# Moving the sums of the state and the split of the first h from GpSimd to VectorE and ScalarE, in a gated graph network with an attention layer behind it

## Chip, cores, metric

One core of a Trainium2 chip. The metric is the device time of one run in microseconds (us).

## The reference, cut

64 graphs of 256 nodes with 256 features. Per graph: layer norm and ReLU, three gated steps, a residual sum, layer norm and ReLU again, one attention layer, a residual sum.

```python
h = jnp.maximum(_layernorm(x), 0.0)
for i in range(3):                                   # gated steps
    m = jnp.einsum('bnd,de->bne', h, weight[i])
    aggr = jnp.einsum('bst,bsd->btd', A, m)          # A: the adjacency, 0 or 1
    h = gru(aggr, h)                                 # two products with 256 x 768, sigmoid, tanh
x = x + h
h = jnp.maximum(_layernorm(x), 0.0)
hW = jnp.einsum('bnd,od->bno', h, W)
e = leaky((hW @ a_left)[:, :, None] + (hW @ a_right)[:, None, :])
x = x + softmax(where(A == 0, -1e9, e)) @ hW
```

## The kernel before

Two graphs are one pair; 32 pairs, of which up to three are in flight. Each operation is recorded with an engine and a guessed duration. A list scheduler then places them one by one, the one that can start first in its model first, by deadline where several can, and issues them in that order. Each engine has its own list, so the scheduler fixes who stands behind whom; the chip decides how long each takes. `pool` and `dve2` (VectorE operations with two inputs in SBUF, among others) are marked: in its model the scheduler never lets one of each run at the same time. Nothing makes the chip keep the modelled times, and in the trace they do overlap.

A product with the gate weights is done with seven half-size products in place of eight (Strassen-Winograd), which needs sums of quarters of its right factor. The right factors are h ("the sums of the state") and the aggregate; the first were on GpSimd, the others on VectorE:

```python
def right_factors(eng, op, b):
    T = Buf("full")
    c = (1195, 605, 605) if eng is nc.gpsimd else (V512, V256, V256)
    def first():
        q = quarters(b)
        eng.tensor_sub(T.t[:, : 2 * N].rearrange("p (c n) -> p c n", c=2), q[:, :, 1, :],   # L381
                       b.t[:, : 2 * N].rearrange("p (c n) -> p c n", c=2))
    op(c[0], first, ...)
    op(c[1], lambda: eng.tensor_sub(quarter(T, T2), quarter(b, B22), quarter(T, T1)), ...)  # L385
    op(c[2], lambda: eng.tensor_sub(quarter(T, T4), quarter(T, T2), quarter(b, B21)), ...)  # L387
    return T
```

The aggregate is a product of rounded tiles: h = hi + lo, both rounded, times the adjacency (L521 on TensorE, evicted by ScalarE at L525). For the first h the split was GpSimd's; for later ones it comes out of PSUM, hi by ScalarE (L583), lo by VectorE (L585).

```python
pool(530, lambda ...: nc.gpsimd.tensor_copy(nodes(hi)[:, sl, :], nodes(h)[:, sl, :]), ...)       # L504
pool(1190, lambda ...: nc.gpsimd.tensor_sub(nodes(lo)[:, sl, :], nodes(h)[:, sl, :],
                                            nodes(hi)[:, sl, :].bitcast(F32)), ...)                # L506
for i in range(L):
    Th = right_factors(nc.gpsimd, pool, hT)
    ...                                               # L521, L525: the aggregate
    Tg = right_factors(nc.vector, dve2, agT)
    ...                                               # products L413, evictions L420, additions L423
    dve2(...)   # L551  u = (u + b) * r       two SBUF inputs
    dve2(...)   # L554  u = u + u'            two SBUF inputs
    act(...)    # L556  tanh
    dve2(...)   # L558, L559, L561  h = (h - u) * z + u, in place
    ...         # L575 transposes of the new h; L583, L585 its split
```

In the attention layer, per pair: transposes of the softmax (L644), eviction by VectorE (L648), a product (L653), eviction by ScalarE (L657), the last projection (L662), all in the same lists as the gated steps of the two pairs behind it. The changed kernel is two lines shorter above these, so L662 is L660 there, L551 is L549, and so on.

## Time and profile before

| | before |
|---|---|
| time, median of 3 | 2404.17 us (2400.3 to 2406.48) |
| span of the profiled run | 2403.4 us |
| steady pair | 73.03 us, repeated within 0.01 |
| TensorE / VectorE / ScalarE / GpSimd busy | 98 / 73 / 56 / 22% |

A busy share of TensorE says little of what a change is worth. The useful count is this: take the distance from the end of one matrix instruction to the end of the next, subtract the usual distance of its kind (the prediction gives the three); what is left is a stop, with what the first instruction behind it loses. Below, "stop" always means this number, and stops per steady pair are means over 20 pairs. Lines from the profile before stand in the prediction.

### The profile page before, as it was taken

The numbers are of one execution on the slowest core, as the hardware profiler recorded it, in microseconds if no ns is written. First come the engines' busy times: TensorE is split into PE (matmuls) and PEld (weight loads), VectorE is DVE, ScalarE is ACT, GpSimd is POOL, SyncE is SP. The second block draws the span as 40 slices with busy tenths as digits, with TensorE's granted clock in tenths as the row PEclk, the third lists the DMA queues.
The fourth block names the chain that finished last, engine by engine and source line by source line (L and its number), as shares of the span: only waits on it lengthen the run. The fifth ranks groups of instructions, "written<-read, shape, count | busy, mean of one in ns | idle before, by whom it ended". The sixth has DMA issues, their size and how long they took to land.

```text
span 2403.4 us, 32216 instructions
## 1 busy us (share of the span) xinstructions
PE 2352.6 (98%) x12129; PEld 2068.3 (86%) x12129; DVE 1746.6 (73%) x3736; ACT 1352.0 (56%) x2627; POOL 520.3 (22%) x582
## 2 busy tenths in 40 slices
PE   8999999999999999999999999999999999999997
PEld 6878888888888888888888888888888888888885
DVE  5577776787777786777877767877777867778666
ACT  5455555556555556455555555565555564556554
POOL 3031222221222211222212222212222112222110
PEclk9999999999999999999999999999999999999998
DMA  3010000000000000000000000000000000000000
GB/s 114 1 36 1 27 27 27 27 18 10 27 27 27 27 9 18 27 27 27 27 1 27 27 27 27 18 10 27 27 27 27 6 22 27 27 19 9 1 9 18
DMA packets 53564, 55.03 MB, mean 23 GB/s; under 512 B 1680, under 2 KB 53408, under 8 KB 53408
## 3 DMA queue, kind: packets, MB, share of 16 engines
q1 hardware_dynamic: 53376, 52.96, 6.6%
q8 instruction: 96, 1.57, 0.3%
q14 instruction: 60, 0.49, 0.1%
q10 hardware_dynamic: 32, 0.01, 0.0%
HBM read 36.18 MB, written 16.78 MB: 22 GB/s over the span
## 4 chain that ended last, share of the span: by engine, by line
PE 88%; DVE 8%; ACT 3%; issue 0%; DMA 0%; POOL 0%; ACTq 0%; DVEq 0%
PE bank L413 69%; PE bank L521 8%; PE bank L662 5%; PE bank L575 3%; DVE full L551 3%; ACT full L556 2%; DVE full L554 1%; DVE full L648 1%; PE bank L482 1%; PE bank L644 1%; ACT full L657 1%; PE bank L611 1%; PE bank L653 1%; PE bank L345 0%; DVE full L423 0%
## 5 line engine op out<-in xcount | busy, mean ns | idle before, releaser
L413 PE MATMUL bank<-full,fac_hh 128*128 128x256 f32 x4032 | 1002.3, 379 | 0.6 <-ACT full L486 0.2
L413 PE MATMUL bank<-full,fac 128*128 128x256 f32 x4032 | 992.0, 379 | 0.0
L413 PEld LDWEIGHTS bank<-full,fac 128*128 128x128 f32 x4032 | 753.8, 190 | 96.6 <-DVE full L385 0.7
L413 PEld LDWEIGHTS bank<-full,fac_hh 128*128 128x128 f32 x4032 | 747.2, 190 | 93.6 <-DVE full L423 0.6
L423 DVE TENSOR_TENSOR full<-full,bank 128x512 f32<-128x512 f32 x576 | 379.9, 681 | 406.8 <-PE bank L413 349.4
L420 ACT COPY full<-bank 128x512 f32<-128x512 f32 x576 | 327.1, 584 | 283.7 <-PE bank L413 283.6
L381 POOL TENSOR_TENSOR full<-full 128x512 f32<-128x512 f32 x96 | 129.7, 1351 | 1204.5 <-DVE full L561 772.4
L537 ACT ACTIVATE full<-full,b_rz 128x512 f32<-128x512 f32 x192 | 131.5, 716 | 204.2 <-DVE full L423 203.9
L521 PE MATMUL bank<-round,round 128*128 128x256 f32 x1536 | 242.9, 301 | 3.4 <-DVE round L585 2.8
L521 PEld LDWEIGHTS bank<-round,round 128*128 128x128 f32 x1536 | 205.1, 190 | 21.7 <-issue 11.5
L462 POOL TENSOR_TENSOR small<-small,nhalf 128x2 f32<-128x2 f32 x128 | 91.8, 726 | 554.3 <-DVE small L460 552.6
L556 ACT ACTIVATE full<-full,vec 128x512 f32<-128x512 f32 x192 | 135.0, 723 | 100.5 <-DVE full L554 98.6
L525 ACT COPY full<-bank 128x512 f32<-128x512 f32 x192 | 112.6, 587 | 138.3 <-PE bank L521 138.3
L469 ACT ACTIVATE full<-x,small 128x256 f32<-128x256 f32 x256 | 136.6, 593 | 65.1 <-DVE small L464 65.0
L551 DVE SCALAR_TENSOR_TENSOR full<-full,vec,full 128x512 f32<-128x512 f32 x192 | 166.7, 895 | 7.2
L554 DVE TENSOR_TENSOR full<-full 128x512 f32<-128x512 f32 x192 | 141.1, 761 | 1.3
L662 PE MATMUL bank<-wT,full 128*128 128x256 f32 x512 | 118.6, 385 | 19.2 <-ACT full L657 19.2
L662 PEld LDWEIGHTS bank<-wT,full 128*128 128x128 f32 x512 | 95.0, 190 | 42.2 <-ACT full L657 30.4
L561 DVE TENSOR_TENSOR full<-full,full 128x512 f32<-128x512 f32 x192 | 127.7, 692 | 2.1
L559 DVE TENSOR_TENSOR full<-full,full 128x512 f32<-128x512 f32 x192 | 127.6, 690 | 1.3
L558 DVE TENSOR_TENSOR full<-full,full 128x512 f32<-128x512 f32 x192 | 127.3, 689 | 0.4 <-ACT full L556 0.4
L583 ACT CAST round<-bank 128x512 fp32r<-128x512 f32 x128 | 69.6, 594 | 101.0 <-PE bank L575 101.0
(79 smaller groups left out, 2282.6 us busy)
## 6 DMA issues: line engine op xcount, KB each, us to landing
x<-in_x_dram SPq DMA_DIRECT2D x32, 512.0 KB, 3.3
adj<-in_adj_dram SPq DMA_DIRECT2D x32, 512.0 KB, 3.3
out_dram<-x SPq DMA_DIRECT2D x32, 512.0 KB, 2.9
full<-in_L_gnn_w_ih_dram SPq DMA_DIRECT2D x2, 384.0 KB, 5.3
full<-in_L_gnn_weight_dram SPq DMA_DIRECT2D x3, 256.0 KB, 7.0
full<-in_L_gnn_w_hh_dram SPq DMA_DIRECT2D x2, 384.0 KB, 6.7
full<-in_L_gnn_W_dram SPq DMA_DIRECT2D x1, 256.0 KB, 7.2
rows<-in_L_gnn_a_dram ACTq DMA_DIRECT2D x1, 2.0 KB
```

Of the source, the lines that this page charges most:

```text
L381: eng.tensor_sub(T.t[:, : 2 * N].rearrange("p (c n) -> p c n", c=2), q[:, :, 1, :], b.t[:, : 2 * N].rearrange("p (c n) -> p c n", c=2))
L413: nc.tensor.matmul(bank.t[:, ts(s, N)], fac[t[0]][:, f, t[1], :], quarter(srcs(t), q), start=(first and n == 0), stop=True, skip_group_che ...
L420: act(A512, lambda: nc.scalar.copy(quarters(dest[e])[:, :, g, :], both(X)), r=[(X, ONE)], w=[(dest[e], (g, 2 + g))])
L423: dve(V512, lambda: nc.vector.tensor_add(quarters(dest[e])[:, :, g, :], quarters(dest[e])[:, :, g, :], both(bank)), r=[(bank, ONE)], w=[(d ...
L469: act(495, lambda k=k, nb=nb: nc.scalar.activation(nodes(dst)[:, k, :], nodes(src)[:, k, :], AF.Relu, bias=sm.t[:, 18 + nb : 19 + nb], sca ...
L521: nc.tensor.matmul(pa.t[:, ts(db, N)], nodes(part)[:, k, ts(db, P)], Ar()[:, k, :], start=(n == 0), stop=(n == len(terms) - 1))
L537: act(630, lambda s=s, RZ=RZ: nc.scalar.activation(feats(RZ[0])[:, s, :], feats(RZ[0])[:, s, :], AF.Sigmoid, bias=b_rz[:, 2 * s : 2 * s + 1]),
L551: dve2(660, lambda u=u, db=db, en=en, RZ=RZ: nc.vector.scalar_tensor_tensor(u(), u(), b_h[:, en : en + 1], feats(RZ[db])[:, 0, :], op0=ALU ...
L554: dve2(V512, lambda u=u, b=U[db]: nc.vector.tensor_add(u(), u(), feats(b)[:, 1, :]), r=[(U[db], (2, 3))], w=[(U[db], (0, 1))])
L556: act(630, lambda u=u, en=en: nc.scalar.activation(u(), u(), AF.Tanh, bias=b_i[:, en : en + 1]), r=[("vec", ONE)], w=[(U[db], (0, 1))])
L561: dve2(V512, lambda u=u, d=d: nc.vector.tensor_add(d(), d(), u()), r=[(U[db], (0, 1))], w=[(hT, q)])
L662: nc.tensor.matmul(pv.t[:, ts(ib, D)], ag.t[:, db * N + ib * P : db * N + (ib + 1) * P], wT[:, db, :], start=(db == 0), stop=(db == DB - 1))
```

## The change

GpSimd should keep only the power operation of the layer norm and a fill; its first sum takes 1351 ns in the mean, VectorE's of the same size 684.

```diff
-    def right_factors(eng, op, b):
+    def right_factors(b):
         T = Buf("full")
-        c = (1195, 605, 605) if eng is nc.gpsimd else (V512, V256, V256)
...
-            eng.tensor_sub(T.t[:, : 2 * N]...
+            nc.vector.tensor_sub(T.t[:, : 2 * N]...
-        op(c[0], first, ...)
+        dve2(V512, first, ...)
...   (the other two sums likewise)
-            pool(530, lambda ...: nc.gpsimd.tensor_copy(nodes(hi)..., nodes(h)...
+            act(630, lambda ...: nc.scalar.copy(nodes(hi)..., nodes(h)...
-            pool(1190, lambda ...: nc.gpsimd.tensor_sub(
+            dve2(V512, lambda ...: nc.vector.tensor_sub(
...
-            Th = right_factors(nc.gpsimd, pool, hT)
+            Th = right_factors(hT)
-            Tg = right_factors(nc.vector, dve2, agT)
+            Tg = right_factors(agT)
```

Every engine's list is scheduled anew from these durations.

More of the change, by code (lines that the diff above doesn't have):

```diff
@@ L373, in tile_gated_gnn_then_gat @@
     quarter = lambda b, q: b.t[:, q * N : (q + 1) * N]
-    def right_factors(eng, op, b):
+    def right_factors(b):
         T = Buf("full")
-        c = (1195, 605, 605) if eng is nc.gpsimd else (V512, V256, V256)
         def first():
             q = quarters(b)
-            eng.tensor_sub(T.t[:, : 2 * N].rearrange("p (c n) -> p c n", c=2), q[:, :, 1, :],
+            nc.vector.tensor_sub(T.t[:, : 2 * N].rearrange("p (c n) -> p c n", c=2), q[:, :, 1, :],
                            b.t[:, : 2 * N].rearrange("p (c n) -> p c n", c=2))
-        op(c[0], first, r=[(b, (B11, B12, B22))], w=[(T, (T1, T3))])
-        op(c[1], lambda: eng.tensor_sub(quarter(T, T2), quarter(b, B22), quarter(T, T1)),
+        dve2(V512, first, r=[(b, (B11, B12, B22))], w=[(T, (T1, T3))])
+        dve2(V256, lambda: nc.vector.tensor_sub(quarter(T, T2), quarter(b, B22), quarter(T, T1)),
            r=[(b, (B22,)), (T, (T1,))], w=[(T, (T2,))])
-        op(c[2], lambda: eng.tensor_sub(quarter(T, T4), quarter(T, T2), quarter(b, B21)),
+        dve2(V256, lambda: nc.vector.tensor_sub(quarter(T, T4), quarter(T, T2), quarter(b, B21)),
            r=[(b, (B21,)), (T, (T2,))], w=[(T, (T4,))])
@@ L503, in pair @@
             sl = slice(g * NB, (g + 1) * NB)
-            pool(530, lambda sl=sl, hi=hi, h=h: nc.gpsimd.tensor_copy(nodes(hi)[:, sl, :], nodes(h)[:, sl, :]),
+            act(630, lambda sl=sl, hi=hi, h=h: nc.scalar.copy(nodes(hi)[:, sl, :], nodes(h)[:, sl, :]),
                  r=[(h, ks)], w=[(hi, ks)])
-            pool(1190, lambda sl=sl, hi=hi, lo=lo, h=h: nc.gpsimd.tensor_sub(
+            dve2(V512, lambda sl=sl, hi=hi, lo=lo, h=h: nc.vector.tensor_sub(
                 nodes(lo)[:, sl, :], nodes(h)[:, sl, :], nodes(hi)[:, sl, :].bitcast(F32)),
```

## The prediction

> **What bounds the kernel now.** I read the page first: busy shares, then the slices.
>
> ```profile
> PE 2352.6 (98%) x12129; PEld 2068.3 (86%) x12129; DVE 1746.6 (73%) x3736; ACT 1352.0 (56%) x2627; POOL 520.3 (22%) x582
> ...
> PE   8999999999999999999999999999999999999997
> DVE  5577776787777786777877767877777867778666
> ```
>
> TensorE is busy in all slices but the first and last. VectorE has some 650 us free, GpSimd 1880 us. So taking work off GpSimd frees no engine that sets the time; the change can only gain where TensorE stands still or starts late. I therefore ask what the change is worth at those places alone. Next view: the chain that ended last, in order of time, in one steady pair of graphs (the loop runs 32 pairs).
>
> ```profile
> 1033.08 0.68 DVE full L648
> 1033.76 2.34 DVE full L551 x2
> 1036.10 1.15 DVE full L554
> ...
> 1037.92 0.72 ACT full L556
> 1038.65 0.48 ACT full L657
> 1039.13 0.04 issue
> 1039.17 3.72 PE bank L662 x16
> ...
> 1049.12 28.49 PE bank L413 x132
> ```
>
> The last line gives TensorE's undisturbed pace: 28.49/132 = 0.216 us per 256-column matrix instruction. From the individual records I took the distance from one end to the next for every line (0.216 us for 256 columns of fp32, 0.119 for the products of the rounded tiles at L521, 0.109 for transposes at 128) and added up what lies above the median: 71.8 us in all, so a perfect TensorE stream would take some 2332 us. By stretches of 73.05 us, the length of one pair: 7.5, 4.0 and 7.3 us in the first three; 1.21 us in each of the next 27; about 1 us in each of the next two; 19.5 us in the tail. Of the 1.21 us, 0.96 stands at L662 (0.69 idle, then a first instruction that is 0.27 longer), 0.25 at L521. Hence the ceiling: 27 to 28 steady pairs hold about 34 us, the start 19, the tail 19.5. The view of who waited for whom agrees:
>
> ```profile
> PE bank L662 <- ACT full L657: 19.2, 28, 0.7
> ```
>
> The wait's cause is further back: the eviction L657 stands on ScalarE behind two tanh (L556), which wait for VectorE's L551 and L554. Timeline of that spot, after a clean spot from earlier in the same pair:
>
> ```profile
> 1005.14 1.41 DVE L551 SCALAR_TENSOR_TENSOR full<-full,vec,full 128x512 f32<-128x512 f32 x2
> 1006.47 1.28 DVE L554 TENSOR_TENSOR full<-full 128x512 f32<-128x512 f32 x2
> ```
>
> ```profile
> 1033.67 2.42 DVE L551 SCALAR_TENSOR_TENSOR full<-full,vec,full 128x512 f32<-128x512 f32 x2
> ...
> 1034.16 1.38 POOL L381 TENSOR_TENSOR full<-full 128x512 f32<-128x512 f32 x1 [14.68 <-ACT full L486]
> ...
> 1035.62 1.06 POOL L385 TENSOR_TENSOR full<-full,full 128x256 f32<-128x256 f32 x1
> 1036.02 1.81 DVE L554 TENSOR_TENSOR full<-full 128x512 f32<-128x512 f32 x2
> ```
>
> The same two pairs of instructions take 2.69 us in the clean spot, 4.1 beside GpSimd's sums of the first h. That is the finding the prediction rests on. Sorting all records by overlap with GpSimd: L551 takes 748 ns alone (136 times), 1251 with overlap (56); L554 684 alone, 1172 with overlap (30). L423, which reads one operand from PSUM, takes 682 and 680: no difference.
>
> **What the Trainium skill says.** "SBUF — State Buffer", section "SBUF: two separate sides": GpSimd and VectorE share a port pair that is "an exclusive lock, not a bandwidth split", against VectorE operations with two SBUF inputs or in a two-port mode. The trace agrees: L551 and L554 (two SBUF inputs) stretch by 0.5 us, L423 (one PSUM input) not. "GPSIMD Engine Reference", section "Elementwise — side-by-side cycle accounting": an fp32 two-input sum is 1.96 times slower on GpSimd. The trace: 1351 ns against 684 at L381, a ratio of 1.98. "Trainium Kernel Development and Optimization", section "Performance Expectations", calls matmul busy time a bad metric; indeed 98% hides nothing here, but says nothing of the 0.27 us after a stop, so I counted distances between ends.
>
> **The change part by part.** Durations by line and form:
>
> ```profile
> L381 POOL TENSOR_TENSOR full<-full 128x512 f32<-128x512 f32 x96 | 129.7, 1351 | 1204.5 <-DVE full L561 772.4 <-ACT full L486 416.5 <-PE bank L482 15.6
> L506 POOL TENSOR_TENSOR round<-full,round 128x512 fp32r<-128x512 f32 x64 | 82.0, 1281 | 5.1
> L385 POOL TENSOR_TENSOR full<-full,full 128x256 f32<-128x256 f32 x96 | 80.6, 839 | 7.5
> L387 POOL TENSOR_TENSOR full<-full,full 128x256 f32<-128x256 f32 x96 | 69.2, 735 | 3.0
> L504 POOL CAST round<-full 128x512 fp32r<-128x512 f32 x64 | 39.8, 622 | 83.8 <-ACT full L469 83.7
> ```
>
> - GpSimd loses these five: 129.7 + 82.0 + 80.6 + 69.2 + 39.8 = 401 us; 520 - 401 = about 119 us stay (power 92, fill 30).
> - VectorE gains 96 x (0.684 + 0.424 + 0.424) = 147 us of sums (its own L381, L385, L387 without overlap) and 64 x 0.68 = 44 us (as L585): +191.
> - VectorE loses the stretching. L551: 56 x 0.50 = 28; L554: 30 x 0.49 = 15; the six of L558, L559, L561 near 151 us: 4.6; the factor sums in setup 3.3; the rest some 3: -54. Net 1747 + 137 = 1884 us, 78%.
> - ScalarE gains 64 casts. A 384-element SBUF copy takes 0.51 to 0.53; 128 elements more at 0.86 ns (L302: 372 to 482 ns from 256 to 384) make 0.63: +40 us, 58%.
> - TensorE: same instructions, and in the order listing of the two builds the steady pair has nearly the same order.
>
> On the path: at the L662 spot VectorE's new order is the same two copies, two L551, two L554 and only then a new sum. By hand: first L551 at 1033.67, both in 1.33 us of pitch, so L554 from 1035.0; the first ends at 1035.7, and tanh starts at 1035.8 instead of 1037.27. Two tanh and the first eviction end near 1037.8. TensorE asks for it at 1038.48 (1039.17 less 0.69). Slack 0.7 us: the wait goes, 0.96 us x 28 = **27 us**.
>
> Is a new wait put in? Following the new order on, per pair: the sum ahead of the two instructions before L662 ends near 1036.9, needed at 1037.6; the updated h is complete near 1040.5, needed for transposes at 1041.9; the split's low half for the next L521 near 1044.2, needed at 1044.8; the new h's first sums near 1044.9 against 1043.5 on GpSimd, used 3 us and more later. All hold, two by only 0.6 us. The 0.25 us at L521 I leave. In the start, the stretched VectorE work is again on the path:
>
> ```profile
> 153.74 2.76 DVE L559 TENSOR_TENSOR full<-full,full 128x512 f32<-128x512 f32 x2
> ...
> 158.22 0.47 PE L575 MATMUL bank<-ident,full 128*128 128x128 f32 x1 [3.15 <-DVE full L561]
> ```
>
> There and at the waits of 1.65 and 0.92 us before L521 near 53 and 84 us, up to 8 us hang on stretching (with the slower clock after a stop). But here VectorE also takes new sums in between, and the order is new: I count **3 us**. In the tail TensorE and ScalarE keep their order and the last GpSimd sum lies at 2330 us: 0. Sum 27 + 3 = 30: 2404 - 30 = **2374 us**.
>
> **The rivals.** (a) VectorE becomes the bound: 137 us more work, additions at L423 come later and hold PSUM banks. Against it: 78% busy, 19 us idle of 73 in a pair, of which the new work takes about 4.3; the profile shows almost no TensorE wait on L423 (0.6 us in the start of weight loads). For it: one in-order queue, two slacks of 0.6 us. If each pair got a new 1 us stop: 2400 us; two: 2430. (b) The gain is hidden: the wait at L662 only moves to the next dependence, at L575 or L521. Then the middle gives 10 us instead of 27: 2390. (c) All stops of the middle and the contention in the start go: 34 + 8 = 42 us: 2362. (d) GpSimd's slower sums were themselves on the path and TensorE speeds up by 400 us: impossible, as only 71.8 us stand above the pace.
>
> **Range and chances.** The ceiling, 72 us with 19.5 in a tail that hardly changes, leaves 52: over 2% (below 2357) needs 47 of these 52. 0.05. Slower by over 2% needs 1.5 us of new stops per pair on top of losing the gain: 0.02. Range: from (c) with a little, 2362, to between (b) and (a), 2394.
>
> **What would show it.** Right: L551 and L554 near 748 and 684 ns throughout, L662's wait for L657 gone, a pair's period of 72.1 us instead of 73.05, GpSimd near 120 us, VectorE near 1880. Wrong: a new steady wait of TensorE on a VectorE sum or addition, or the period unchanged while L551 is clean (rival b). If the start moves by more than 6 us either way, my 3 us was the mis-sized term.

## The result

2378.75 us (2377.68 to 2379.53, 5 runs) against 2404.17; ratio 0.9894, 95% interval 0.9879 to 0.9908. Ratios in this document are the mean time of one kernel's runs over that of the other's of the same rounds, so not quite the ratio of the medians. The gain is about 1%; 2374 was predicted.

The page of the changed kernel, busy shares and then groups (busy us, mean ns of one | idle before):

```profile
PE 2341.7 (99%) x12129; PEld 2067.1 (87%) x12129; DVE 1862.3 (78%) x4088; ACT 1389.2 (58%) x2691; POOL 130.7 (6%) x166
...
L549 DVE SCALAR_TENSOR_TENSOR full<-full,vec,full 128x512 f32<-128x512 f32 x192 | 138.3, 747 | 7.8 <-DVE full L421 0.5
L379 DVE TENSOR_TENSOR full<-full 128x512 f32<-128x512 f32 x192 | 131.8, 686 | 10.4 <-ACT full L523 6.5
...
L552 DVE TENSOR_TENSOR full<-full 128x512 f32<-128x512 f32 x192 | 126.6, 686 | 1.3
```

Before, the group that is L549 here read:

```profile
L551 DVE SCALAR_TENSOR_TENSOR full<-full,vec,full 128x512 f32<-128x512 f32 x192 | 166.7, 895 | 7.2
```

VectorE's busy time grew by 116 us, not by the 191 of the moved work, above all since L549 and L552 now run at 747 and 686 ns (895 and 761 in the mean before). The chain in order of time, one steady pair:

```profile
1021.84 0.86 PE bank L411 x4
1022.70 3.45 PE bank L660 x16
...
1032.39 28.49 PE bank L411 x132
...
1065.21 0.96 PE bank L519 x8
1066.17 0.02 issue
1066.20 0.59 ACT full L523
1066.79 0.12 issue
1066.91 1.19 PE bank L519 x8
```

At L660 the chain runs from TensorE to TensorE: the stop before the last projection is gone. It leaves TensorE at one place only, before the second L519 of one gated step. Before the change that place had a stop of 0.26 us, now 0.56 (0.59 as a mean, since two of the 20 pairs had a longer one). The place in the timelines, before and after:

```profile
1003.75 1.28 DVE L423 TENSOR_TENSOR full<-full,bank 128x512 f32<-128x512 f32 x2 [1.14 <-PE bank L413]
...
1009.48 0.68 DVE L585 TENSOR_TENSOR round<-bank,round 128x512 fp32r<-128x512 f32 x1
...
1010.27 1.01 PEld L521 LDWEIGHTS bank<-round,round 128*128 128x128 f32 x8 [0.39 <-issue]
```

```profile
1060.02 0.42 DVE L385 TENSOR_TENSOR full<-full,full 128x256 f32<-128x256 f32 x1
...
1060.36 1.28 DVE L421 TENSOR_TENSOR full<-full,bank 128x512 f32<-128x512 f32 x2
...
1066.08 0.69 DVE L583 TENSOR_TENSOR round<-bank,round 128x512 fp32r<-128x512 f32 x1
1066.20 0.59 ACT L523 COPY full<-bank 128x512 f32<-128x512 f32 x1 [1.02 <-PE bank L519]
...
1066.88 1.01 PEld L519 LDWEIGHTS bank<-round,round 128*128 128x128 f32 x8 [0.69 <-ACT full L523]
```

Before, VectorE was idle and began the additions as soon as TensorE had finished their banks. Now it is still in the last sum of h (L385), and the additions, the tanh inputs and the low half of the split follow later. The page names ScalarE's L523 as what the second L519 waited for; that ends at 1066.79, but VectorE's second L583 ends at 1066.77, and the program makes this L519 read just that low half. Which of the two it is, and whether the sum is to blame, the experiments had to say.

Where the time came from, by the start of the last projection in the second pair (235.9 us before, 226.0 after), 27 pairs after it, and the rest:

| stretch | before | after | gain | predicted |
|---|---|---|---|---|
| start | 235.9 | 226.0 | 9.9 | 3 |
| 27 pairs | 1971.7 | 1955.0 | 16.7 | 27 (counted with 28) |
| tail | 195.8 | 194.9 | 0.9 | 0 |
| span | 2403.4 | 2375.9 | 27.5 | 30 |

### The profile page after: what moved, and what is told of

Same layout as the page of the kernel before. It is cut to its first block, busy times and chain, and to the rows that moved or that the text cites. A ratio compares the mean times of both kernels' runs of the same rounds, so it can differ in the third digit from the quotient of the medians.

```text
span 2375.9 us, 32083 instructions
## 1 busy us (share of the span) xinstructions
PE 2341.7 (99%) x12129; PEld 2067.1 (87%) x12129; DVE 1862.3 (78%) x4088; ACT 1389.2 (58%) x2691; POOL 130.7 (6%) x166
## 4 chain that ended last, share of the span: by engine, by line
PE 94%; DVE 4%; ACT 1%; issue 0%; DMA 0%; POOL 0%; ACTq 0%; DVEq 0%
PE bank L411 71%; PE bank L519 8%; PE bank L651 5%; PE bank L660 4%; PE bank L573 3%; PE bank L642 1%; PE bank L480 1%; ACT full L523 1%; DVE full L421 1%; PE bank L609 1%; PE bank L345 0%; DVE full L549 0%; DVE full L552 0%; DVE full L556 0%; DVE full L557 0%
## 5 line engine op out<-in xcount | busy, mean ns | idle before, releaser
L421 DVE TENSOR_TENSOR full<-full,bank 128x512 f32<-128x512 f32 x576 | 380.7, 683 | 274.4 <-PE bank L411 265.1
L418 ACT COPY full<-bank 128x512 f32<-128x512 f32 x576 | 326.9, 584 | 208.6 <-PE bank L411 208.6
L519 PE MATMUL bank<-round,round 128*128 128x256 f32 x1536 | 240.7, 299 | 9.5 <-ACT full L523 8.3
L519 PEld LDWEIGHTS bank<-round,round 128*128 128x128 f32 x1536 | 202.8, 189 | 26.2 <-ACT full L523 19.7
L460 POOL TENSOR_TENSOR small<-small,nhalf 128x2 f32<-128x2 f32 x128 | 99.8, 789 | 2026.3 <-DVE small L458 2023.3
L523 ACT COPY full<-bank 128x512 f32<-128x512 f32 x192 | 112.7, 587 | 159.3 <-PE bank L519 111.1
L554 ACT ACTIVATE full<-full,vec 128x512 f32<-128x512 f32 x192 | 135.0, 723 | 66.1 <-DVE full L552 64.2
L549 DVE SCALAR_TENSOR_TENSOR full<-full,vec,full 128x512 f32<-128x512 f32 x192 | 138.3, 747 | 7.8 <-DVE full L421 0.5
L379 DVE TENSOR_TENSOR full<-full 128x512 f32<-128x512 f32 x192 | 131.8, 686 | 10.4 <-ACT full L523 6.5
L559 DVE TENSOR_TENSOR full<-full,full 128x512 f32<-128x512 f32 x192 | 126.6, 689 | 2.1
L552 DVE TENSOR_TENSOR full<-full 128x512 f32<-128x512 f32 x192 | 126.6, 686 | 1.3
L556 DVE TENSOR_TENSOR full<-full,full 128x512 f32<-128x512 f32 x192 | 126.2, 685 | 0.4 <-ACT full L554 0.4
L538 ACT ACTIVATE full<-bank,b_rz 128x256 f32<-128x256 f32 x192 | 82.8, 466 | 69.0 <-PE bank L411 68.7
L651 PE MATMUL bank<-full,full 128*128 128x256 f32 x512 | 117.8, 383 | 0.2 <-DVE full L646 0.2
```

Source lines behind the costliest of these rows:

```text
L379: nc.vector.tensor_sub(T.t[:, : 2 * N].rearrange("p (c n) -> p c n", c=2), q[:, :, 1, :], b.t[:, : 2 * N].rearrange("p (c n) -> p c n", c=2))
L418: act(A512, lambda: nc.scalar.copy(quarters(dest[e])[:, :, g, :], both(X)), r=[(X, ONE)], w=[(dest[e], (g, 2 + g))])
L421: dve(V512, lambda: nc.vector.tensor_add(quarters(dest[e])[:, :, g, :], quarters(dest[e])[:, :, g, :], both(bank)), r=[(bank, ONE)], w=[(d ...
L519: nc.tensor.matmul(pa.t[:, ts(db, N)], nodes(part)[:, k, ts(db, P)], Ar()[:, k, :], start=(n == 0), stop=(n == len(terms) - 1))
L523: act(A512, lambda g=g, pa=pa, agT=agT: nc.scalar.copy(quarters(agT)[:, :, g, :], pa.t.rearrange("p (c n) -> p c n", c=DB)), r=[(pa, ONE)] ...
L549: dve2(660, lambda u=u, db=db, en=en, RZ=RZ: nc.vector.scalar_tensor_tensor(u(), u(), b_h[:, en : en + 1], feats(RZ[db])[:, 0, :], op0=ALU ...
```

## The experiments

Theory: GpSimd's two-input sums held up VectorE's two-input instructions ahead of a wait of TensorE; the change takes that away, and in exchange puts a sum of h into VectorE's queue that costs 0.3 us per pair. Rivals: the split carries the gain; the new order does; the sums being done sooner does; any relief of GpSimd does.

| run | median us | ratio to before, 95% | steady pair us | stops in it, us |
|---|---|---|---|---|
| before | 2404.17 | 1 | 73.03 | 0.95 L662, 0.26 L521 |
| changed | 2378.75 | 0.9894 (0.9879 to 0.9908) | 72.42 | 0.59 L519 |
| split only | 2399.88 | 0.9987 (0.9972 to 1.0003) | 73.03 | 0.96 L662, 0.26 L521 |
| sums only | 2382.3 | 0.9912 (0.9893 to 0.9931) | 72.38 | 0.55 L519 |
| sums back, same order | 2417.36 | 1.0061 (1.0045 to 1.0077) | 73.58 | 0.95 L660, 0.81 L519 |
| idle sums added | 2489.54 | 1.0361 (1.0344 to 1.0378) | 76.05 | 2.57 aggregate, 1.66 products |
| idle fills added | 2378.0 | 0.9888 (0.9873 to 0.9903) | 72.38 | 0.55 aggregate |
| sums yield | 2516.92 | 1.0464 (1.0447 to 1.0482) | 77.40 | 3.52 products, 1.18 L609, 0.85 L519 |
| low half first | 2449.97 | 1.0187 (1.0172 to 1.0202) | 74.88 | 1.34 L642, 1.48 L651, 0.18 products |
| both of these | 2457.82 | 1.0216 (1.0198 to 1.0233) | 74.98 | much the same |
| fourth sum later | 2369.38 | 0.9849 (0.9835 to 0.9862) | 72.10 | 0.27 aggregate |
| low half swapped | 2362.53 | 0.9820 (0.9807 to 0.9833) | 71.84 | 0.02 |

All gave correct results. "Aggregate" is the line L519 of the changed kernel, where an experiment's edit shifts line numbers.

### One part of the change alone

Split only: the second part of the diff above, put on the kernel before.

> Only the split of the first h leaves GpSimd; the sums of the state stay there. Contention theory (the gain is that the GpSimd sums no longer stretch the two-input VectorE work ahead of the tanh and of the last projection L662): the sums still run beside L551, so the stop before the last projection stays, 0.9 to 1.0 us in every steady pair, the period stays at 73.0 to 73.1 us, and only the start gains: 2394 to 2404 us. Rival (the gain comes of the split, or of any work taken off GpSimd): 2376 to 2388 us.

2399.88 us. The steady pair is that of the kernel before; only the start is shorter (230.5 us in place of 235.9 up to the last projection of the second pair), while the tail is 1.2 us longer. In the total this gain is not clear of noise: the interval of the ratio includes 1. The 5.4 us are read from one profile of each kernel.

Sums only: the first part of the diff.

> Only the sums of the state move to VectorE; the split stays on GpSimd. Contention theory: the stop before the last projection is gone in every steady pair, the period is 72.3 to 72.6 us, 2374 to 2386 us. Rival (the split carries the gain): 2394 to 2404 us.

2382.3 us, the period and the stop of the changed kernel; start 231.3 us. So the middle belongs to the sums alone. In the start the two parts give 5.4 and 4.6 us, and both together 9.9: in these single profiles they add up.

### Is it the order, or the contention?

Sums back, same order. The scheduler still plans the sums of h as VectorE's; only the instruction issued is GpSimd's:

```diff
-    def right_factors(b):
+    def right_factors(b, eng=nc.vector):
...
-            nc.vector.tensor_sub(T.t[:, : 2 * N]...      (and the other two)
+            eng.tensor_sub(T.t[:, : 2 * N]...
...
-            Th = right_factors(hT)
+            Th = right_factors(hT, nc.gpsimd)
```

The lists of TensorE and ScalarE were compared with the changed kernel's and are the same. As the scheduler does not know of these sums on GpSimd, it does not keep them apart from VectorE's operations, as it did in the kernel before.

> The changed kernel with the sums of the state issued on GpSimd again, while the scheduler plans as if they were on VectorE: the order on TensorE and ScalarE, and of everything else on VectorE, is that of the changed kernel, instruction for instruction. Contention theory: L549 and L552 are stretched again in some 50 places, the stop before the last projection returns (0.6 to 1.0 us per steady pair), the stop before the second L519 falls from 0.56 to about 0.25 us; period 72.7 to 73.1, 2388 to 2402 us. Rival (the new order of instructions made the gain): period 72.4, 2376 to 2382 us.

2417.36 us, slower than expected and slower than before. The view of who waited for whom:

```profile
PE bank L660 <- ACT full L655: 19.2, 28, 0.7
```

It is the line of the kernel before to the last digit. The order is not the gain. The stop before the second L519 fell to 0.26 us, as expected with no sum of h on VectorE. The miss is a third stop of 0.56 us, before another L519: there GpSimd's sum also holds up one of VectorE's sums of the aggregate (L383 at 1.38 us in the chain, 0.42 undisturbed), and a low half behind it comes late. That is read from the chain of this run and not tested further; the planning that no longer keeps the two engines apart may be why it was not there before.

Idle sums added. In the changed kernel GpSimd does three sums of h as well, into a tile that nobody reads; they are issued with the first sum on VectorE and are no operation of the plan, so all other lists stay (and the scheduler does not keep them apart from VectorE's operations):

```diff
+            if extra:      # for h only
+                nc.gpsimd.tensor_sub(scratch.rearrange("p (c n) -> p c n", c=2), q[:, :, 1, :],
+                                     b.t[:, : 2 * N].rearrange("p (c n) -> p c n", c=2))
+                nc.gpsimd.tensor_sub(scratch[:, :N], quarter(b, B22), quarter(b, B11))
+                nc.gpsimd.tensor_sub(scratch[:, N:], quarter(b, B22), quarter(b, B21))
```

> The changed kernel with three two-input GpSimd sums of the same sizes added for each set of sums of h, which write a tile that nobody reads; the order on all other engines is unchanged. Contention theory: L549 is stretched by 0.5 us in some 50 places as before the change, the stop before the last projection returns, and the stop before the second L519 stays at 0.5 or more: period 73.0 to 73.6, 2392 to 2420 us. Rival (the gain is that the sums themselves are done sooner on VectorE, whatever GpSimd does): period 72.4, 2376 to 2382 us.

2489.54 us, 69 above the expected range. Two groups of it (line L556 is L549 of the changed kernel):

```profile
L556 DVE SCALAR_TENSOR_TENSOR full<-full,vec,full 128x512 f32<-128x512 f32 x192 | 166.6, 895 | 7.8 <-DVE full L428 0.9
...
L382 POOL TENSOR_TENSOR scratch<-full 128x512 f32<-128x512 f32 x96 | 146.8, 1529 | 1330.1 <-DVE full L566 866.9 <-ACT full L491 433.7 <-issue 29.5
```

The stretching is back: 895 ns in the mean, as before the change, and 747 without. That the stop would return at the last projection was wrong: TensorE now stops right ahead of it, at a product (L418) that needs VectorE's first sum of h (L386), and again before the aggregates:

```profile
PE bank L418 <- DVE full L386: 39.9, 29, 1.4
```

Work whose result nobody reads cost 111 us. The rival that the gain came of the sums being done sooner is not excluded by this run, as VectorE's sums of h come late here too, behind the held-up gate operations. Two other things speak against it: in the kernel before, no wait of TensorE for a sum on GpSimd is in the list of waits; and a run below puts one sum of h later and gains.

Idle fills added: the same trigger, but GpSimd copies two columns of h, so that it waits for h in the same way, and fills the tile five times.

```diff
+                nc.gpsimd.tensor_copy(scratch[:, :2], quarter(b, B22)[:, :2])
+                for _ in range(5):
+                    nc.gpsimd.memset(scratch, 0.0)
```

> As the run with idle sums, but at the same trigger GpSimd copies two columns of h (so that it waits for h in the same way) and then fills the scratch tile five times, some 2.5 us in all: as busy, but it hardly reads SBUF. The order on the other engines is again that of the changed kernel. Contention theory (two operands in SBUF on both engines): L549's line is not stretched, period 72.3 to 72.6, 2374 to 2384 us. Rival (GpSimd being busy at all, or its waits for h and the power operations queued behind, made the idle sums' 110 us): 2400 us or more.

```profile
L384 POOL MEMSET scratch<- 128x512 f32 x480 | 252.0, 525 | 27.8
L555 DVE SCALAR_TENSOR_TENSOR full<-full,vec,full 128x512 f32<-128x512 f32 x192 | 138.3, 747 | 7.1
```

2378.0 us: GpSimd is as busy as with the idle sums (425 us against 455), and neither L555's 747 ns nor the time moves. What costs is GpSimd reading SBUF beside VectorE's operations with two SBUF inputs, not GpSimd being busy, nor its waits for h. Two inputs on GpSimd's side, as the expectation had it, are not needed: in the kernel before, near 151 and 154 us, GpSimd's cast L504, which has one input, holds an L558 and an L559 to 1.11 and 1.09 us in place of 0.68, and both end 0.55 us after the cast. The copies of two columns in the run with fills hold nothing up: the 56 L555 beside one took 744 ns in the mean.

### The 0.3 us that the change brings

I first changed the scheduler. Sums yield: a sum of h is placed on VectorE only if no other operation could start within 450 ns.

```diff
-                    if fits and (best is None or (t, o.prio, o.seq) < best[0]):
+                    if fits and (best is None or (t + o.yields, o.prio, o.seq) < best[0]):
...   (yields is 450 for the sums of h, 0 otherwise)
```

> The changed kernel; the scheduler places a sum of h on VectorE only if nothing else of any engine could start within 450 ns. Theory (the stop of 0.56 us before the second L519 is 0.25 plus 0.3 for a sum of h that delays the additions and with them the tanh inputs and the split's low half): the stop falls to 0.25, period 72.0 to 72.15, 2366 to 2374 us. Rival (the 0.3 us has another cause, as the place of the split's low half behind the first update of h): the stop stays, 2376 to 2382 us, or the new order brings other stops.

2516.92 us; pairs alternate between 68.3 and some 86 us. The sums now come too late: TensorE waits 60.2 us in 14 places for the first sum (L379), in products. It says nothing of the 0.3 us. The clock granted to TensorE was lower as well (0.975 against 0.996).

Low half first: the same field, -1 for L583 alone, so that it wins ties.

> The changed kernel; the scheduler lets the subtraction for the low half of the split state (L583) win ties on VectorE, so that both halves stand ahead of the second tanh input and of the update of h. Theory (TensorE's second L519 waits for VectorE's second L583, though the profile names a ScalarE eviction that ends 0.02 us later): the stop before L519 goes wholly, period 71.8 to 71.9, 2360 to 2368 us, unless the later tanh inputs make a new stop. Rival (it does wait for the ScalarE eviction): stop and time unchanged, 2376 to 2382 us.

Half a hit. The stop before L519 went wholly, which speaks for VectorE's L583 and against the eviction that the profile names. But both low halves now stand ahead of the tanh inputs, the whole list was planned otherwise, and new stops of 1.3 and 1.5 us per pair came at the attention's transposes and product (L642 for ScalarE's exponentials, L651 for VectorE's L646). In the longer pairs (75.97 us against 74.28) some eight instructions behind the stop at L651 also stand 0.43 us apart in place of 0.216, so a stop can cost more than its length; the granted clock of this run was 0.989. 2449.97 us.

> Both scheduler edits at once. Theory: no more than the better of the two in the middle (period 71.8 to 71.9), 2358 to 2368 us; the start and the tail may differ by a few us either way.

2457.82 us: the same stops. Both misses have one lesson: an edit to a greedy scheduler is no edit to one place.

So the last two leave the plan as it is, and move single operations in the finished order, just before it is issued (with assertions that no dependence is broken; the lists of TensorE and ScalarE are unchanged):

```diff
-            o.fn()
             order.append(o)
...
+        dve = [o for o in order if o.eng == "DVE"]
+        tags = [o.tag for o in dve]
+        for n in range(len(dve) - 14):       # fourth sum later
+            if tags[n : n + 7] == ["sum1", "sum2", "sum4", "add", "add", "gate", "gate"]:
+                low = [m for m in range(n, n + 16) if tags[m] == "low"]
+                if len(low) == 2:
+                    behind(dve[n + 2], dve[low[1]])
+        for o in order:
+            o.fn()
```

Here "sum4" is L385 (the last sum), "add" L421, "gate" L549, "low" L583.

> The changed kernel, planned as it is; only then, at some 29 places, the last of the three sums of h (0.42 us), which stands ahead of two additions, is put behind the second subtraction for the low half. Theory (this sum delays the additions, and everything behind them, by some 0.3 us): the stop before the second L519 falls from 0.56 to 0.2 to 0.3 us, period 72.0 to 72.15, 2367 to 2374 us. Rival (the 0.3 us comes of something else): period 72.4, 2376 to 2382 us.

2369.38 us, as expected: the stop falls from 0.56 to 0.27 us, its size before the change. The sum of h ahead of the additions is the cause of the 0.3 us.

The last run has this loop in place of the first, again on the planned order of the changed kernel:

```diff
+        for n in range(len(dve) - 3):        # low half swapped
+            if tags[n : n + 4] == ["low", "update", "update", "low"]:
+                before(dve[n + 3], dve[n + 1])
```

> The changed kernel, planned as it is; only then, at some 29 places, VectorE's second subtraction for the low half of the split state is put ahead of the two first instructions of the update of h that stand before it. All other orders stay. Theory (TensorE's second L519 waits for that subtraction, although the profile names a ScalarE eviction): the stop of 0.56 us goes, no other comes, period 71.8 to 71.9, 2360 to 2368 us. Rival (it waits for the eviction, or a new stop comes as with the rescheduled version): 2374 us or more.

2362.53 us, ratio 0.982 to the kernel before: faster than the changed kernel and than the run with the fourth sum later. TensorE did wait for VectorE's L583 there, not for the eviction. The chain at the same place (L536 is L519 of the changed kernel) no longer leaves TensorE:

```profile
1058.84 0.95 PE bank L536 x8
1059.79 0.43 PE bank L428 x2
1060.22 0.95 PE bank L536 x8
```

A steady pair has 0.02 us of stops left; what stands above TensorE's pace in the whole run is 28.5 us, nearly all in the start and the tail.

## Why the prediction was right, point by point

- That the ceiling is what stands above TensorE's pace, not GpSimd's 401 us: right. 71.8 us stood above before, 44.2 after; the difference, 27.6, is the gain in span, 27.5.
- That the stop before the last projection hangs on L551 and L554 being held up by GpSimd, and goes: right, and now shown by four runs: it stays with the split alone and comes back with the sums on GpSimd in the new order; it is gone with the sums alone moved and with idle fills. It was worth 0.95 us in each of 28 places, as worked out.
- That a mean of 1251 ns describes L551 with overlap: the mean hid two kinds. By single records, 164 of the 192 took about 0.75 us and 28 about 1.75, one in each steady pair. The first L551 of a couple was already running and ran on; the second began 0.17 us after GpSimd's sum and ended 0.55 us after the sum's end. The first L554 behind it likewise took 1.21 us and ended 0.55 us after GpSimd's next sum. The sum of 28 us is the same, but this is blocking, not slowing.
- Two readings were loose. The couples of L551 and L554 were added up where clean (2.69 us) and taken from start to end beside the sums (4.1); both from start to end they are 2.62 and 4.16. The ratio of 1.98 has in it GpSimd sums that were held up themselves; the 34 that met no two-input operation of VectorE took 1273 ns, 1.87 times VectorE's 681.
- That no new wait comes in the middle, and L521 stays at 0.25 us: wrong, and this is the term that was mis-sized. Its stop rose to 0.56 to 0.59 us, which turned 27 us into 16.7. The step that failed is the walk through VectorE's new order: it followed one stretch of the pair, behind L662, and called the rest held. The stop was in another gated step, where VectorE used to stand idle ahead of an addition and now finishes a sum. It is rival (a) in small: 0.3 us in each pair where it had named 1.
- That the start gives 3 us: mis-sized the other way, 9.9. The prediction saw "up to 8 us" hang on stretching and then took most of it back for the new sums and the new order. Near 150 us the six updates of h took 8.3 us before, 1.1 to 1.75 us each; now they take 4.9 with two low-half subtractions (0.69 us each) among them. The last two, before and after:

```profile
156.42 2.88 DVE L561 TENSOR_TENSOR full<-full,full 128x512 f32<-128x512 f32 x2
```

```profile
151.85 1.29 DVE L559 TENSOR_TENSOR full<-full,full 128x512 f32<-128x512 f32 x2
```

Counted as stops, what the prediction had seen nearly all went: 7.1 us between 153 and 163 us, around the transposes behind these updates, became 0.5; 1.9 us near 53 us became 0; 1.2 us near 84 us became 0.4. The slower clock that it speaks of is there: the transposes behind the first stop stand 0.213 us apart, and the granted clock from 133 to 206 us was 0.95, against 1.00 after the change.

- The tail, 0 predicted: 0.9 us. VectorE 1884 us predicted, 1862 measured; ScalarE 1392 and 1389; GpSimd 119 and 131; the period 72.1 and 72.4.

Two errors of the sum, -10 and +7, all but cancel: the mechanism was right, but that 2374 came so near to 2378.75 with two wrong sizes is in part luck.

What stays open: which of GpSimd's operations held up how much of the start. The runs only split the 9.9 us between the two parts of the change.

## What to carry to other kernels

Where one engine is busy nearly all the time, add up its stops and look at what stands at the head of each; moving work off an idle engine can still pay, if that work blocks instructions on the way to a stop. When an operation joins an in-order queue, look for the place where that queue used to wait idle for the bottleneck engine, as there even 0.3 us is paid in full. A wait's label in a profile with two candidates ending 0.02 us apart is a guess: swap one of them and see.

## What the Trainium skill lacked or had wrong

- "SBUF — State Buffer", section "Who interferes with whom": nothing wrong. It says that a VectorE instruction with two SBUF inputs contends with a GpSimd one that reads SBUF, not with one that only writes it, and the runs agree: 895 ns in the mean with the idle sums, 747 with 480 fills. It has no number for a VectorE sum blocked by a GpSimd one: here a blocked instruction took 1.75 us in place of 0.75 and ended 0.55 us after GpSimd's.
- "Perfetto Trace Analysis", section "Optimizing Scalar/DVE Operations": it says that offloading between the two "might not help". Here it did harm: the same sums of h on GpSimd, with TensorE and ScalarE in the same order, took 38.6 us more than on VectorE (2417.36 against 2378.75).
- No page says how to judge a wait whose two candidates end within 0.02 us. Here the label named ScalarE (1066.79 us) where VectorE (1066.77 us) was the cause; putting that one instruction earlier took the stop from 0.56 to 0.02 us.
